# Two attentions on one core: one pair of value products moved in front of a step's second maxima, the other left behind its scores

## The chip, the core and the metric

The kernel runs on one core of a Trainium2 chip. A core has a matrix engine (TensorE, PE in the profile), three engines for elementwise work (VectorE or DVE, ScalarE or ACT, GpSimd or POOL), a queue that issues transfers (SP), an SBUF memory of 128 partitions and a PSUM memory of 128 partitions by 8 banks into which TensorE writes. The metric is the device time of one execution in microseconds (us), the median of several runs.

## The reference

The input is 16 sequences of 512 rows of 128 numbers. Four layers are applied one after the other, each to the layer norm of what came before it, and each added back: a causal attention of 16 heads of 8 numbers with a bias and a projection, a mixture of 8 experts of which two are taken per row, an attention of 16 heads without mask and projection, and a gated layer of width 352 with inputs and weights quantized to four-bit values. Only the attentions matter here:

```python
w = jnp.einsum('bhnd,bhmd->bhnm', q, k) * jax.lax.rsqrt(float(D))
w = jnp.where(mask > 0, w, NEG)          # first attention only
w = jax.nn.softmax(w, axis=-1)
attn = jnp.einsum('bhnm,bhmd->bhnd', w, v)
```

## The kernel before

Both attentions are one function, `attention`. Its unit of work is a *group* (batch b, group g): 16 batches of four groups, each of four heads. The four heads are numbered by a pair index i (0 or 1) and a half j (0 or 1); j says on which 64 partitions of `q` and `k` the head lies. A group takes four *steps*, kc = 0 to 3, one for each block of 128 keys.

In a step TensorE does three kinds of work, always in the order in which the program issues it (`mm` and `in_order`, line 294, tie each matmul to the one before).

- *Maxima* (`row_max`, its reduction is line 911): scores of one block of 128 queries, queries as rows, for a group three ahead (LEAD = 3), into a PSUM tile `ps_max` of two banks. VectorE reduces it to the largest score of each row. `ps_max`, `ps_d`, and in the first attention `ps_qk`, `ps_v` and others share a ring of two such tiles (`for_dve`). In the first attention a bf16 product with a mask follows each.
- *Scores* (`score`): scores of a block of keys against the queries, keys as rows, in one-bank tiles `ps_sc`. The maxima have been put into spare rows of `q`, so they are already subtracted. ScalarE takes the exponential of each tile into `pt` in SBUF (line 177), and in the first attention GpSimd clears what lies above the diagonal (line 969). `ps_sc`, `ps_av`, `ps_t`, `ps_mx`, and in the second attention `ps_qk` and `ps_v`, share a ring of four one-bank tiles (`for_act`).
- *Value products* (`attend`): `pt` times the values, for four heads, each 128 rows by 32 columns of the array, written to 32 partitions of one bank, `ps_av`, summed over the group's four steps. When the group is done, `leave` copies `ps_av` to SBUF on ScalarE, and later `divide` turns it back (`ps_d`) and divides.

Maxima and scores each come in `parts`: one part for each pair index i, thus two a step in the second attention, with 512 columns for each head. In the first attention only the causal part is computed; blocks of 512 and 384 columns (kc = 0 and 1) come in two parts, those of 256 and 128 (kc = 2 and 3) in one that holds both pairs.

The loop at the end of `attention` writes the order of a step out by hand. Small work that is due at a step (layer norm, turns, queries and keys, values, the gate) is kept in three tables by step: `soon` is done first, `later` after the first maxima and first scores, `last_of` after the second. A list `behind` holds work one step late: the value products of step kc are done at the end of the next step, when their exponentials have had time. So before the change a step is: `soon`; first maxima; first scores; (in step kc = 2 of the first attention, `divide`); `later`; second maxima; second scores; `last_of`; the four value products of the step before; at a group's end also `leave`. `last_of` holds the first attention's queries and keys (`both`, step 10 of 16), and in the second attention `divide` (step kc = 2).

Of the kernel before, what the change touches and what calls it, by code (L numbers as in the profile page):

```python
# [36 lines left out]
def transformer_kernel(  # L37
# [24 lines left out]
    B, S, E = x_in.shape  # L62
    NC = S // P
# [88 lines left out]
    def in_order(ins, queue="pe", passing=False):  # L152


        if queue in last:
            tc.add_manual_dep(
                ins.ins, last[queue].name,
                mybir.DependencyInfo(
                    mybir.DependencyClass.NoSync, mybir.DependencyReason.DATA
                ),  # L160
                reason="in_order",
            )
        if not passing:
            last[queue] = ins.ins
        return ins
# [127 lines left out]
    def mm(out, lhsT, rhs, start=True, stop=True):  # L293
        return in_order(nc.tensor.matmul(out, lhsT, rhs, start=start, stop=stop))  # L294
# [263 lines left out]
    def attention(layer):  # L558
# [25 lines left out]
        NP = 8  # L584
# [6 lines left out]
        def for_act(name):  # L591
            return ring["act"](name)
# [294 lines left out]
        def strip(j):  # L887
            return slice(64 * j, 64 * (j + 1))
# [52 lines left out]
        def main_parts(b, g):  # L941


            hv = halves[b, g // 2]
            va = state[b]["va"]
            pts = {}
            acc = {}

            def score(kc, pairs):
                q0 = kc * P if causal else 0  # L950
                n = S - q0
                m = len(pairs)
                tiles = [for_act("ps_sc") for j in range(2)]
                for u, i in enumerate(pairs):
                    p = 2 * (g % 2) + i
                    for j, ps in enumerate(tiles):
                        r = strip(j)
                        mm(
                            ps[:, u * n : (u + 1) * n],
                            hv["k"][r, p, kc * P : (kc + 1) * P], hv["q"][r, p, q0:S],  # L960
                        )
                for j, ps in enumerate(tiles):
                    pt = pool.tile([P, S], F32, tag="pt", name="pt", bufs=12 if causal else 8)
                    act.activation(pt[:, 0 : m * n], ps[:, 0 : m * n], AF.Exp, scale=SCALE)
                    if causal:

                        head = pt[:, 0 : m * n].rearrange("p (u n) -> p u n", u=m)[:, :, 0:P]
                        in_order(
                            nc.gpsimd.affine_select(  # L969
                                head, head, pattern=[[0, m], [1, P]], base=0,  # L970
                                channel_multiplier=-1, compare_op=ALU.is_ge, fill=0.0,
                            ),
                            queue="pool",
                        )
                    for u, i in enumerate(pairs):
                        pts[kc, i, j] = pt[:, u * n : (u + 1) * n]

            def attend(kc):
                if kc == 0:
                    acc[0] = for_act("ps_av")  # L980
                av = acc[0]
                q0 = kc * P if causal else 0
                for i in range(2):
                    for j in range(2):
                        s = 2 * j + i
                        mm(
                            av[32 * s : 32 * (s + 1), q0:S],
                            va[:, kc, NP * j + 2 * g + i, :],
                            pts.pop((kc, i, j)),
                            start=kc == 0, stop=kc == NC - 1,  # L990
                        )

            def leave():
                t = pool.tile([P, S], F32, tag="av_sb", name="av_sb")
                act.copy(t, acc.pop(0))
                return t

            return score, attend, leave

        def divide(b, g, t):  # L1000

            st = state[b]
            if g == 0:
                st["at"] = pool.tile([P, NC, E], F32, tag="at", name="at")
            ps = for_dve("ps_d")[:, 0, :]
            for c in range(NC):
                cols = slice(c * P, (c + 1) * P)
                turn_to(ps[:, cols], t[:, cols])
            p3 = ps.rearrange("p (n k) -> p n k", k=32)
            rec = pool.tile([P, NC * 4, 1], F32, tag="rec", name="rec")  # L1010
            vec.reciprocal(rec, p3[:, :, D : D + 1])
            at = st["at"].rearrange("p c (j n d) -> p (c j) (n d)", j=2, d=D)
            vec.tensor_tensor(
                at[:, :, 2 * D * g : 2 * D * (g + 1)].rearrange("p m (i d) -> p m i d", d=D),
                p3[:, :, 0:D].rearrange("p (m i) d -> p m i d", i=2),
                rec.rearrange("p (m i) o -> p m i o", i=2).to_broadcast([P, NC * 2, 2, D]),
                ALU.mult,
            )

        def turn_back(b):  # L1020
            if causal:
                state[b]["aT"] = transposed(pool, for_act, state[b]["at"], "aT", act.copy)
# [28 lines left out]
        def parts(blocks):  # L1051

            return [(0, 1)] if causal and 2 * blocks * P <= S else [(0,), (1,)]

        def max_steps(n):
            if n >= len(groups):
                return []
            b, g = groups[n]
            return [
                [(lambda c=c, u=u: row_max(b, g, c, u)) for u in parts(c + 1)]  # L1060
                for c in reversed(range(NC))
            ]
# [130 lines left out]
        behind, left = [], []  # L1193
# [53 lines left out]
        def quantize_after(b, step):  # L1247

            f = fp4_steps(b)
            for name, d in (  # L1250
                ("stats", 2), ("moments", 4), ("apply", 5), ("largest", 6), ("scale", 8),
                ("inverse", 10), ("scaled", 12), ("size", 14), ("least", 15), ("down", 15), ("grid", 16),
            ):
                later.setdefault(step + d, []).append(f[name])

        for n, (b, g) in enumerate(groups):
            nxt = n + LEAD
            steps = max_steps(nxt)
            score, attend, leave = main_parts(b, g)
            for kc in range(NC):  # L1260
                now = NC * n + kc
                maxima = steps.pop(0) if steps else []
                scores = [lambda u=u: score(kc, u) for u in parts(NC - kc)]
                for f in soon.pop(now, []):
                    f()
                if maxima:
                    maxima.pop(0)()
                scores.pop(0)()
                if kc == 2 and left:
                    bb, gg, t = left.pop(0)  # L1270
                    if not causal:
                        last_of.setdefault(now, []).append(lambda a=(bb, gg, t): divide(*a))
                    else:
                        divide(bb, gg, t)
                    if gg == G - 1 and causal:
                        later.setdefault(now + 1, []).append(lambda bb=bb: turn_back(bb))
                        at = now + 3
                        later.setdefault(at, []).append(lambda bb=bb: finish(bb))
                        gate_after(bb, at)
                    elif gg == G - 1:  # L1280
                        soon.setdefault(now + 1, []).append(lambda bb=bb: finish(bb))
                        quantize_after(bb, now + 1)
                for f in later.pop(now, []):
                    f()
                for f in maxima + scores:
                    f()
                for f in last_of.pop(now, []):
                    f()

                while behind:  # L1290
                    behind.pop(0)()
                behind.append(lambda kc=kc, f=attend: f(kc))
            behind.append(lambda b=b, g=g, f=leave: left.append((b, g, f())))
            max_done(nxt, NC * (n + 1))
        while behind:
# [290 lines left out]
    def gated_ffn():  # L1586
# [136 lines left out]
        fctx.close()  # L1723

    attention(0)

    later_pool = ctx.enter_context(tc.tile_pool(name="grids", bufs=1))
    grids = [later_pool.tile([P, NC, E], BF16, name=f"grid{b}") for b in range(B)]
    scales = [later_pool.tile([P, S // BLOCK, 1], F32, name=f"scale{b}") for b in range(B)]
    attention(1)  # L1730
    gated_ffn()

# [64 lines left out]
```

## Time and profile before

| | |
|---|---|
| median of 3 runs | 2253.49 us (2253.28 to 2253.72) |
| the profiled execution's own time | 2251.99 us |
| its span, first to last instruction | 2250.3 us |
| TensorE clock granted, mean | 0.964 of full |
| first attention, steady part | about 100 to 820 us |
| second attention | about 1220 to 2025 us |

The kernel's span has, in order, some 70 us of loading and the first attention's start, the first attention, the experts, the second attention, and the gated layer. In the profile's lines a group of instructions is named by engine, source line, operation and tile: `ps_av<-pt,va 128*32 128x512` is a product into `ps_av` that uses 128 rows and 32 columns of the array and streams 512 columns. In a listing by time, the first number is the start, the second the time until the end of the last of the merged instructions, `x8` how many there are; what stands in brackets is idle time of the engine ahead of it and what ended it. An fp32 matmul on TensorE leaves two records, so that four value products are `x8`.

### The profile page before, as it was taken

How to read it: one execution, taken by the hardware profiler on the slowest of the kernel's cores; microseconds unless marked ns; L12 is line 12 of the kernel's file. 1: busy time of each engine (PE TensorE's matmuls, PEld its weight loads, DVE VectorE, ACT ScalarE, POOL GpSimd, SP SyncE). 2: the span in 40 equal slices, each digit the busy share in tenths (PEclk: the TensorE clock that was granted, in tenths of full speed). 3: DMA queues.
4: the chain of work that ended last, by engine and by line, in shares of the span. 5: the costliest groups of instructions: out<-in, count | busy, mean ns of one | idle time of the engine just before them, and what ended most of it. 6: DMA issues, size and time to landing. Idle time of an engine off the chain costs nothing.

```text
span 2250.3 us, 38218 instructions
## 1 busy us (share of the span) xinstructions
PE 2025.0 (90%) x13140; PEld 1018.6 (45%) x13140; DVE 1649.7 (73%) x2994; ACT 1298.3 (58%) x2564; POOL 1022.3 (45%) x1641
## 2 busy tenths in 40 slices
PE   6999999999999965989998999999999999995887
PEld 3444444444444433655665433333333333333665
DVE  6667676777767757946434888888888888845887
ACT  1566556656556642323334777777777777782443
POOL 3444646566574663132202345555455454215554
PEclk6999999999999977999999999999999999997999
DMA  7311222322222103554553222322222222100000
GB/s 195 110 60 60 77 81 86 95 73 74 66 76 84 57 27 100 152 157 140 160 147 95 69 69 80 92 80 73 85 69 68 69 69 68 59 2 0 24 24 28
DMA packets 148736, 180.15 MB, mean 80 GB/s; under 512 B 25647, under 2 KB 112784, under 8 KB 140352
## 3 DMA queue, kind: packets, MB, share of 16 engines
q1 hardware_dynamic: 139614, 160.26, 23.8%
q0 software_dynamic: 8352, 17.20, 2.6%
q8 instruction: 105, 1.72, 0.3%
q14 instruction: 87, 0.71, 0.1%
q10 hardware_dynamic: 578, 0.26, 0.1%
HBM read 116.55 MB, written 58.99 MB: 78 GB/s over the span
## 4 chain that ended last, share of the span: by engine, by line
PE 37%; DVE 14%; ACT 4%; POOL 2%; issue 1%; DMA 0%; ACTq 0%; POOLq 0%
PE ps_av L294 10%; PE ps_sc L294 6%; PE ps_max L294 6%; DVE mx L911 5%; PE ps_h L294 4%; PE ps_y L294 4%; DVE hid L177 4%; ACT pt L177 3%; PE ps_d L297 2%; PE ps_qk L294 1%; POOL hid L177 1%; DVE f_mx L177 1%; PE ps_t L297 1%; DVE ml L177 1%; PE ps_v L294 1%
## 5 line engine op out<-in xcount | busy, mean ns | idle before, releaser
L911 DVE TENSOR_REDUCE mx<-ps_max 128x2 f32<-128x1024 f32 (+1 forms) x896 | 1005.4, 1144 | 259.4 <-PE ps_max L294 255.0
L177 ACT ACTIVATE pt<-ps_sc 128x512 f32<-128x512 f32 (+2 forms) x1792 | 895.9, 571 | 443.5 <-PE ps_sc L294 414.4
L294 PE MATMUL ps_sc<-q,k 64*128 64x512 f32 (+3 forms) x2048 | 480.9, 405 | 33.8 <-ACT pt L177 32.1
L294 PE MATMUL ps_av<-pt,va 128*32 128x512 f32 (+3 forms) x4096 | 482.5, 531 | 11.5 <-POOL pt L969 8.1
L294 PE MATMUL ps_max<-k,q 64*128 64x512 f32 (+3 forms) x2048 | 426.8, 433 | 26.3 <-DVE mx L911 19.2
L294 PEld LDWEIGHTS ps_max<-k,q 64*128 64x128 f32 x2048 | 185.9, 188 | 442.6 <-issue 174.6
L969 POOL TENSOR_SCALAR_AFFINE_SELECT pt<-pt 128x128 f32<-128x128 f32 (+1 forms) x768 | 245.8, 331 | 291.6 <-ACT pt L177 275.5
L294 PEld LDWEIGHTS ps_sc<-q,k 64*128 64x128 f32 x2048 | 230.6, 186 | 184.5 <-ACT pt L177 119.2
L1490 ACT ACTIVATE h<-ps_h,b1t 128x512 f32<-128x512 f32 x156 | 106.8, 687 | 192.3 <-PE ps_h L294 191.9
L1414 POOL DMA_INDIRECT got<-y_rows,backs x128 | 123.3, 964 | 99.3 <-DMA y_rows<-yt 63.4
L204 POOL TENSOR_TENSOR ln_rstd<-ln_ve,mhalf 128x4 f32<-128x4 f32 x62 | 63.7, 1028 | 204.2 <-DVE ln_nm L177 180.1
L294 PE MATMUL ps_y<-w2t,h 128*128 128x128 f32 x1248 | 149.6, 279 | 6.9 <-DVE yt L1504 6.9
L294 PE MATMUL ps_h<-xT,w1t 128*128 128x512 f32 x312 | 150.5, 615 | 3.0 <-issue 1.4
L294 PEld LDWEIGHTS ps_y<-w2t,h 128*128 128x128 f32 x1248 | 145.4, 195 | 9.6 <-DVE yt L1504 7.4
L294 PEld LDWEIGHTS ps_av<-pt,va 128*32 128x32 f32 x4096 | 86.5, 108 | 137.0 <-issue 79.5
L533 POOL DMA_INDIRECT x_rows<-xg,slots x128 | 126.6, 989 | 25.7 <-issue 21.6
L294 PE MATMUL ps_max<-mask_bf,ident_bf 128*128 128x128 bf16 (+1 forms) x768 | 126.9, 248 | 0.0
L177 DVE SCALAR_TENSOR_TENSOR hid<-f_a,hid 128x704 f32<-128x704 f32 x64 | 78.6, 1230 | 22.5 <-ACT f_a L177 22.4
L297 PE MATMUL ps_d<-cst,av_sb 128*128 128x128 f32 x512 | 84.1, 287 | 6.6 <-DVE mx L911 5.1
L294 PEld LDWEIGHTS ps_h<-xT,w1t 128*128 128x128 f32 x312 | 50.7, 191 | 77.1 <-ACT h L1490 52.0
L294 PE MATMUL ps_gu<-wgT,xqT 128*128 128x352 f32 x128 | 54.1, 506 | 32.7 <-DVE hid L177 32.7
L177 ACT COPY av_sb<-ps_av 128x512 f32<-128x512 f32 x128 | 76.3, 596 | 11.6 <-PE ps_av L294 2.8
(242 smaller groups left out, 2137.5 us busy)
## 6 DMA issues: line engine op xcount, KB each, us to landing
q<-d SPq DMA_DIRECT2D x256, 128.0 KB
k<-d SPq DMA_DIRECT2D x256, 128.0 KB
d<-hi SPq DMA_DIRECT2D x64, 256.0 KB
d<-lo SPq DMA_DIRECT2D x64, 256.0 KB
xt<-x_rows SPq DMA_DIRECT2D x39, 262.0 KB
w1t<-in_w_dram SPq DMA_DIRECT2D x39, 256.0 KB
w2t<-in_w_dram SPq DMA_DIRECT2D x39, 256.0 KB
y_rows<-yt SPq DMA_DIRECT2D x39, 256.0 KB
```

What stands on the lines that cost most here:

```text
L177: ins = f(*args, **kw)
L204: in_order(nc.gpsimd.tensor_tensor(rstd, ve, mhalf, ALU.pow), queue="pool")
L294: return in_order(nc.tensor.matmul(out, lhsT, rhs, start=start, stop=stop))
L297: return in_order(nc.tensor.transpose(out, src, ident))
L533: ins = in_order(nc.gpsimd.indirect_dma_start(out=x_rows[:, :], out_offset=bass.IndirectOffsetOnAxis(ap=slots[:, b0 + u, k, c : c + 1], axis=0
L911: nc.vector.tensor_reduce(hv["mx"][:, c, :, p0 : p0 + m], s4, AX.X, ALU.max),
L969: nc.gpsimd.affine_select(head, head, pattern=[[0, m], [1, P]], base=0, channel_multiplier=-1, compare_op=ALU.is_ge, fill=0.0,),
L1414: ins = in_order(nc.gpsimd.indirect_dma_start(out=got[:, c, :], out_offset=None, in_=y_rows[0 : min(NT, NE * (b + 1)) * TS, :], in_offset= ...
L1490: nc.scalar.activation(h[:, f, :], ps, AF.Gelu, bias=t["b1"][:, f : f + 1])
```

## The change

`attend` gets the pair index as an argument and does two products instead of four. A step's `behind` list now holds two entries (and `leave` at a group's end). The first is taken out behind `later` and in front of the second maxima, all others behind the second scores; `last_of` moves behind them. A step is now: `soon`; first maxima; first scores; (`divide`); `later`; two value products (i = 0) of the step before; second maxima; second scores; two value products (i = 1), at a group's end `leave`; `last_of`. In the steps kc = 2 and 3 of the first attention, which have no second part, the four products still stand side by side. In the program as built, the value products form 508 bursts of four before; after it 763 bursts of two and 127 of four, the rest at the edges. The instructions themselves, their number, their shapes and the transfers are the same.

```diff
-            def attend(kc):
-                if kc == 0:
+            def attend(kc, i):
+                if kc == 0 and i == 0:
                     acc[0] = for_act("ps_av")
                 av = acc[0]
                 q0 = kc * P if causal else 0
-                for i in range(2):
-                    for j in range(2):
-                        s = 2 * j + i
-                        mm(
-                            av[32 * s : 32 * (s + 1), q0:S],
-                            va[:, kc, NP * j + 2 * g + i, :],
-                            pts.pop((kc, i, j)),
-                            start=kc == 0, stop=kc == NC - 1,
-                        )
+                for j in range(2):
+                    s = 2 * j + i
+                    mm(
+                        av[32 * s : 32 * (s + 1), q0:S],
+                        va[:, kc, NP * j + 2 * g + i, :],
+                        pts.pop((kc, i, j)),
+                        start=kc == 0, stop=kc == NC - 1,
+                    )
...
                 for f in later.pop(now, []):
                     f()
+
+
+                if behind:
+                    behind.pop(0)()
                 for f in maxima + scores:
                     f()
+                while behind:
+                    behind.pop(0)()
                 for f in last_of.pop(now, []):
                     f()
-
-                while behind:
-                    behind.pop(0)()
-                behind.append(lambda kc=kc, f=attend: f(kc))
+                behind += [lambda kc=kc, f=attend, i=i: f(kc, i) for i in range(2)]
             behind.append(lambda b=b, g=g, f=leave: left.append((b, g, f())))
```

More of the change, by code (lines that the diff above doesn't have):

```diff
@@ L1284, in attention @@
                     f()
+                if behind:
+                    behind.pop(0)()
                 for f in maxima + scores:
-                    f()
-                for f in last_of.pop(now, []):
                     f()
@@ L1291, in attention @@
                     behind.pop(0)()
-                behind.append(lambda kc=kc, f=attend: f(kc))
+                for f in last_of.pop(now, []):
+                    f()
+                behind += [lambda kc=kc, f=attend, i=i: f(kc, i) for i in range(2)]
             behind.append(lambda b=b, g=g, f=leave: left.append((b, g, f())))
```

## The prediction, made before the changed kernel had run

> **What bounds the kernel now.** I read the busy times first, then the table of stages, then single steps in order of time, then the waits. Of the page and of the table of stages (busy us of each engine with its instructions, then TensorE clock, DMA share, GB/s):
>
> ```profile
> PE 2025.0 (90%) x13140; PEld 1018.6 (45%) x13140; DVE 1649.7 (73%) x2994; ACT 1298.3 (58%) x2564; POOL 1022.3 (45%) x1641
> ...
> L294 PE MATMUL ps_av<-pt,va 128*32 128x512 f32 (+3 forms) x4096 | 482.5, 531 | 11.5 <-POOL pt L969 8.1
> ```
>
> ```profile
> 100.00:820.00 720.00, 689.69 (x5326) 331.73 (x5324) 501.25 (x1100) 436.06 (x961) 408.29 (x970) 0.99 0.23 73
> 1220.00:2025.00 805.00, 756.70 (x4646) 300.98 (x4646) 678.04 (x1019) 621.44 (x1189) 364.25 (x408) 1.00 0.22 69
> ```
>
> The rows are the two attentions: TensorE is busy 96% and 94% of them, at nearly full clock, with VectorE at 70% and 84%. What the change touches is TensorE's queue alone, so I price it by the distance from one start in that queue to the next (ends are modelled, starts are not). One plain step of the second attention:
>
> ```profile
> 1622.28 0.50 PE L294 MATMUL ps_max<-k,q 64*128 64x512 f32 x2
> 1622.62 0.39 PE L294 MATMUL ps_sc<-q,k 64*128 64x512 f32 x2
> 1622.85 0.40 PE L294 MATMUL ps_max<-k,q 64*128 64x512 f32 x2
> 1623.08 0.39 PE L294 MATMUL ps_sc<-q,k 64*128 64x512 f32 x1
> 1623.69 0.49 PE L294 MATMUL ps_sc<-q,k 64*128 64x512 f32 x1 [0.23 <-ACT pt L177]
> 1624.11 1.07 PE L294 MATMUL ps_av<-pt,va 128*32 128x512 f32 x8
> 1625.11 0.50 PE L294 MATMUL ps_max<-k,q 64*128 64x512 f32 x2
> ```
>
> The step is 2.83 us. The fourth score starts 0.61 us after the third where two scores otherwise start together: its PSUM bank comes free only when ScalarE has done the step's first exponential (four banks, one held by ps_av). That is the stall the change can fill. The value products take 1.00 us to the next start. How are those eight records spread? Narrow windows of the same view show that, and so does one place in the first attention where only the first two of the four products could run, the others waiting for their mask:
>
> ```profile
> 1624.11 0.64 PE L294 MATMUL ps_av<-pt,va 128*32 128x512 f32 x4
> ```
>
> ```profile
> 764.68 0.62 PE L294 MATMUL ps_av<-pt,va 128*32 128x512 f32 x2
> ...
> 764.68 1.05 PE L294 MATMUL ps_av<-pt,va 128*32 128x512 f32 x4
> ```
>
> Each fp32 product leaves two records. The first passes of all four start within 0.02 us (four in the row of 0.64 us), the second passes 0.45 us later: the four run side by side, each in 32 columns of the array. The lone pair (two, then four records) has the same spacing and lasts 1.05 us, where the four last 1.07. **A pair costs what four cost.**
>
> **Second attention, part by part.** I take one batch, from its start at 1584.15 to the next at 1635.22: 51.07 us, 16 steps.
>
> Added: every step gets a second burst of value products, 16 x 0.995 = 15.92 us (0.995 is the distance from ps_av to the next ps_max, in 15 of 16 steps). Changes of shape on the array: in 10 of the steps the scores now precede value products (0.322 us from scores to ps_av) and no longer maxima (0.227), and second maxima follow value products (0.338 to their scores) and no longer scores (0.230): 10 x 0.095 + 9 x 0.11 = 1.9 us. In the other 6 steps a turn, values, queries or maxima's transpose lies there already, so only the burst is new.
>
> Removed: the stalls. In this batch the 12 distances from second scores to ps_av sum to 9.51 us where 12 x 0.322 = 3.86 is bare: 5.64 too much. The 4 in front of ps_d hold 1.13, the one in front of ps_v 0.32; ten from scores to maxima hold 0.83 and one from ps_av to maxima 0.63 (these two on VectorE). Sum 8.55. I take all of it as gone: with a burst of 1.0 us between first and second scores, each score's bank was used by scores one or two half steps of 1.65 us before, and its exponential is done about 1.05 us after them. VectorE needs 1.2 us for a maximum per half step of 1.65.
>
> Net 15.92 + 1.9 - 8.55 = +9.3 us a batch. Built from new: 32 half steps of 0.338 + 0.322 + 0.995 = 52.96, and what else the batch holds (four ps_d at 0.585, two ps_qk at 1.056, ps_v 1.088, ps_t 0.585, two ps_mx at 0.534: 7.2) is 60.2, or +9.1. With 9.2 for 61 of the 64 groups (61/4 = 15.25 batches): **+140**. The last three groups have no maxima; their steps of 2.27 to 2.61 become 2 x (0.322 + 0.995) = 2.63: +1.
>
> ps_d, behind the second burst now, costs the same 0.585 there, and its reader on VectorE has a half step until the second next maxima want its PSUM buffer. A new group's ps_av now asks for its bank earlier, and the built program lets it wait for the last exponential of the step before: done about 1.6 us after that score, wanted at 0.32 + 0.995 + 0.34 + 0.32 = 1.97. Nothing, with 0.4 us to spare. ScalarE's copy of the old ps_av still stands behind the second burst. No DMA is moved; the queues of SP, POOL and VectorE keep their order.
>
> **First attention.** Only half of its steps have second maxima: in these the value products are of 128 columns (step 0, 0.356 us to the next start) and 512 columns (step 1, 0.996).
>
> ```profile
> 422.57 0.43 PE L294 MATMUL ps_av<-pt,va 128*32 128x128 f32 x8
> 423.47 0.44 PE L294 MATMUL ps_max<-k,q 64*128 64x384 f32 x2 [0.47 <-DVE mx L911]
> ...
> 424.60 0.44 PE L294 MATMUL ps_max<-k,q 64*128 64x384 f32 x2
> ...
> 425.56 1.07 PE L294 MATMUL ps_av<-pt,va 128*32 128x512 f32 x8
> 426.56 0.38 PE L294 MATMUL ps_max<-k,q 64*128 64x256 f32 x2
> ```
>
> Eight groups from 406.8 (97.7 us) hold these distances. Added: step 0, four plain ones 0.431 + 0.356 - 0.337 + 0.106 = 0.56 each, and four with ps_mx already between, 0.356 each: 3.6. Step 1, six plain ones 0.371 + 0.996 - 0.281 + 0.105 = 1.19 each, two with ps_o between, 0.996 each: 9.1. Together 12.8. Removed: the bank wait in front of the 128-column products, 1.65 (four of eight are 0.36 too long); waits for VectorE's maxima in front of step 2, 2.05 of 3.2 (one alone is 2.9 and keeps 1.15); three smaller kinds within these steps, 2.0; half of the 0.9 in front of step 0; and 0.74 where the queries, now behind their step's value products, no longer wait for ps_d's buffer. Sum 6.9. Added wait: the first pair of step 0 comes some 0.9 us sooner after its mask on POOL. Set against where the masks end now, one group in eight would come 0.8 us too early, the others have 0.27 us or more; behind it on TensorE queue second maxima and scores. Net 12.8 - 6.9 + 0.8 = +6.7 for eight groups, x 61/8 = **+51**.
>
> **A rule of the Trainium skill** weighs in on the pair's price: "TensorE: Matmul & The Clock Gate", section "Measured speedup vs the span model". Its formula, span = one matmul + 4 ns for each further tile, leaves a pair at four's price and so speaks against this change. Its own measurement, three column tiles 2.38 times as fast, means 1.26 matmuls for three, or 0.13 for each further tile; an estimate from it is 1.13 for a pair and 1.39 for four, so 0.81 us against 0.995. By that a batch gains only 16 x (2 x 0.81 - 0.995) + 1.9 - 8.55 = +3.4 and eight groups +2.7, in all +72 and 2325. The lone pair of this trace says 1.05 against 1.07, at the same 512 columns, and I take that.
>
> **Sum.** 140 + 1 + 51 = +192 on the profiled execution's 2251.99 (span 2250.3): 2444. The median of the runs is 1.5 above it: **2445**.
>
> **The rivals.**
> (a) Faster: a pair takes half of four, 0.5 us, because two thirty-two column products share the array's input and not the time. Then the bursts cost nothing more, a batch changes by 1.9 - 8.55 = -6.65 (-101 in all) and eight groups by about -4.1 (-31): 2122. All of the change's sign hangs on that one price: each 0.1 us off it takes 2 x (244 + 61) x 0.1 + 4 = 65 us, so the break-even is near 0.995 - 192/650 = 0.70 us. For it: the records of one pair alone are few. Against: those say 1.05. Chance 3%.
> (b) Packing is less than perfect (0.81, above): 2325. Chance 6%.
> (c) The stalls return elsewhere: exponentials or maxima are late again because their work is merely moved. Then nothing is removed: 15.25 x 17.8 + 7.6 x 13.6 = +375, 2629. For it: ScalarE is 77% busy in the second attention. Against: its 39.3 us a batch spread over 60. Chance 4%.
> (d) The change does not do what it says: the scheduler keeps four together. The built program has 763 bursts of two where there were none, so no chance.
> The forecast's own case has 87%.
>
> **How the numbers follow.** Low end: a pair 0.05 us cheaper (half of 65, -33) and every stall of the first attention gone (2.4 more in eight groups, -18): about 2395. High end: 1 us a batch of stalls stays (+15) and only 4 of 6.9 go in the first attention (+22): about 2480. That leaves out (a), (b), (c) and a little of the main case: below 2 in 10. A measurement of this kernel can tell 0.2% (4.5 us) from no change. Faster 3%, within 0.2% 1%, slower 96%.
>
> **What would show it.** Right: plain steps of the second attention near 3.31 us, with ps_av twice a step, each as four records over 1.05 us, and the next start 0.99 after it; ps_max to the next batch near 60.2; the wait of ps_sc for ScalarE's exponential nearly gone; the first attention's eight groups near 104.4. Wrong: pairs whose second passes start 0.2 us after the first, or maxima that start before 0.9 us; or waits in front of ps_av for masks in more than one group of eight. The part between and behind the attentions should keep its length.

## The result and the profile after

The changed kernel takes 2493.38 us (2489.15 to 2496.74, four runs) against 2253.6: ratio 1.106, 95% interval 1.104 to 1.108. The direction was forecast, but the time lies 13 us above the range; the forecast +192 became +240. The page after, and the two attentions' stages (start:end, length, busy us with instructions of PE, PEld, DVE, ACT and POOL, granted clock, DMA share, GB/s; they lie later now):

```profile
PE 2311.1 (93%) x13140; PEld 1021.2 (41%) x13140; DVE 1678.9 (67%) x2994; ACT 1320.9 (53%) x2564; POOL 1023.3 (41%) x1641
...
L294 PE MATMUL ps_av<-pt,va 128*32 128x512 f32 (+3 forms) x4096 | 842.0, 533 | 9.5 <-POOL pt L969 8.6
```

```profile
100.00:840.00 740.00, 711.60 (x4796) 315.83 (x4794) 464.20 (x975) 394.83 (x861) 367.09 (x871) 0.94 0.22 69
1300.00:2210.00 910.00, 904.17 (x4498) 284.74 (x4498) 689.84 (x996) 603.31 (x1119) 356.73 (x399) 1.00 0.20 62
```

The same 4096 records of value products keep TensorE busy 842 us instead of 482, with nearly the same mean of one (533 ns, 531 before). In the second attention TensorE has almost no idle time left (busy 904 of 910 us). In the first its clock has fallen from 0.99 to 0.94.

By the first ps_v of the second attention (at 1341.8 us, before the change at 1237.8) the changed kernel is 104 us behind, and the rest of the program costs 138 more. The forecast was 51 and 141. So the second attention came as worked out, and the first cost twice as much. A plain step of the second:

```profile
1800.66 0.50 PE L294 MATMUL ps_max<-k,q 64*128 64x512 f32 x2
1800.99 0.40 PE L294 MATMUL ps_sc<-q,k 64*128 64x512 f32 x2
1801.32 1.05 PE L294 MATMUL ps_av<-pt,va 128*32 128x512 f32 x4
1802.30 0.50 PE L294 MATMUL ps_max<-k,q 64*128 64x512 f32 x2
...
1803.94 0.50 PE L294 MATMUL ps_max<-k,q 64*128 64x512 f32 x2
```

A burst of two is four records over 1.05 us, the next start comes 0.98 after it, and a step is 3.28 us. No score of this step waits for its bank.

The first attention has something new where its queries (ps_qk) are made. Ahead, before the change (two pieces of the listing by time), then after it:

```profile
428.70 1.98 PE L294 MATMUL ps_qk<-xnT,wp 128*128 128x512 f32 x4 [0.30 <-DVE mx L911]
430.62 0.85 PE L294 MATMUL ps_av<-pt,va 128*32 128x384 f32 x8
...
433.49 0.50 PE L294 MATMUL ps_max<-k,q 64*128 64x512 f32 x2 [0.39 <-DVE lo L177]
433.92 0.28 PE L294 MATMUL ps_max<-mask_bf,ident_bf 128*128 128x128 bf16 x2
434.13 0.50 PE L294 MATMUL ps_sc<-q,k 64*128 64x512 f32 x2
```

```profile
474.00 0.85 PE L294 MATMUL ps_av<-pt,va 128*32 128x384 f32 x8
474.78 1.98 PE L294 MATMUL ps_qk<-xnT,wp 128*128 128x512 f32 x4
...
479.56 0.70 PE L294 MATMUL ps_max<-k,q 64*128 64x512 f32 x2 [1.17 <-DVE lo L177]
480.20 0.40 PE L294 MATMUL ps_max<-mask_bf,ident_bf 128*128 128x128 bf16 x2
480.53 0.79 PE L294 MATMUL ps_sc<-q,k 64*128 64x512 f32 x2
```

The value products that stood behind the queries stand in front of them now. So the next maxima, which need the PSUM tile that ps_qk fills until VectorE has made `lo` of it, come 0.78 us sooner after ps_qk, and wait that much longer: 1.17 us of idle TensorE instead of 0.39. From there on the matmuls take longer: the scores of 512 columns 0.79 us, not 0.50. Three stretches of the table of busy times around it, with the columns named above:

```profile
469.30:479.70 10.40, 9.23 (x62) 3.74 (x60) 6.53 (x19) 4.69 (x11) 3.88 (x13) 1.00 0.13 49
479.70:489.90 10.20, 10.20 (x40) 3.53 (x40) 4.59 (x7) 3.97 (x8) 4.49 (x9) 0.50 0.48 154
489.90:500.10 10.20, 10.18 (x76) 4.21 (x74) 6.43 (x8) 7.43 (x17) 6.39 (x14) 1.00 0.43 128
```

The clock is half for 10.2 us, and TensorE has 40 records of matmuls where it has 76 next. Between 250 and 830 us the clock is halved eleven times, for 3.4 to 10.2 us each. Nine of these stretches begin 0.1 to 2.1 us after the end of such a wait; the two of 3.4 us begin within 0.3 us after a wait of 1.06 us for a mask.

### The profile page after: what moved, and what is told of

It is laid out like the page before. It is cut to its first block, busy times and chain, and to the rows that moved or that the text cites. A ratio compares the mean times of both kernels' runs of the same rounds, so it can differ in the third digit from the quotient of the medians.

```text
span 2491.8 us, 38219 instructions
## 1 busy us (share of the span) xinstructions
PE 2311.1 (93%) x13140; PEld 1021.2 (41%) x13140; DVE 1678.9 (67%) x2994; ACT 1320.9 (53%) x2564; POOL 1023.3 (41%) x1641
## 4 chain that ended last, share of the span: by engine, by line
PE 48%; DVE 6%; POOL 2%; ACT 1%; issue 0%; DMA 0%; ACTq 0%; POOLq 0%
PE ps_av L294 20%; PE ps_max L294 9%; PE ps_sc L294 5%; PE ps_h L294 4%; PE ps_y L294 4%; DVE hid L177 4%; PE ps_d L297 2%; PE ps_qk L294 1%; POOL hid L177 1%; DVE f_mx L177 1%; PE ps_t L297 1%; PE ps_v L294 1%; PE ps_mx L297 1%; DVE f_rc L177 1%; ACT f_a L177 1%; DVE f_sc L177 1%
## 5 line engine op out<-in xcount | busy, mean ns | idle before, releaser
L911 DVE TENSOR_REDUCE mx<-ps_max 128x2 f32<-128x1024 f32 (+1 forms) x896 | 1021.7, 1146 | 425.5 <-PE ps_max L294 417.9
L177 ACT ACTIVATE pt<-ps_sc 128x512 f32<-128x512 f32 (+2 forms) x1792 | 919.5, 566 | 671.3 <-PE ps_sc L294 663.6
L294 PE MATMUL ps_av<-pt,va 128*32 128x512 f32 (+3 forms) x4096 | 842.0, 533 | 9.5 <-POOL pt L969 8.6
L294 PE MATMUL ps_max<-k,q 64*128 64x512 f32 (+3 forms) x2048 | 450.1, 457 | 19.5 <-DVE lo L177 16.4
L294 PE MATMUL ps_sc<-q,k 64*128 64x512 f32 (+3 forms) x2048 | 398.3, 403 | 4.9 <-ACT pt L177 4.5
L294 PEld LDWEIGHTS ps_av<-pt,va 128*32 128x32 f32 x4096 | 135.6, 109 | 274.0 <-issue 223.2
L294 PEld LDWEIGHTS ps_sc<-q,k 64*128 64x128 f32 x2048 | 187.9, 189 | 89.7 <-issue 35.2
L873 POOL TENSOR_SCALAR q_a<-q_a 128x512 f32<-128x512 f32 x16 | 24.1, 1507 | 149.8 <-ACT q_a L177 149.8
L177 DVE RECIPROCAL rec<-ps_d 128x16 f32<-128x16 f32 x128 | 32.4, 253 | 79.0 <-PE ps_d L297 79.0
```

The lines of the kernel that those rows point to most:

```text
L177: ins = f(*args, **kw)
L873: nc.gpsimd.tensor_scalar(st["a"], st["a"], MAGIC, None, ALU.max), queue="pool"
L911: nc.vector.tensor_reduce(hv["mx"][:, c, :, p0 : p0 + m], s4, AX.X, ALU.max),
```

## The experiments

Two theories for the first attention's surplus: (1) the queries' move makes a wait, and the wait is followed by half clock; (2) bursts that use half of the array bring the clock down. I give the first attention as the time of eight groups in its steady part, twice the mean distance of ps_v over ten batches of four groups there: 98.8 us before, 113.0 after. A batch of the second attention is 50.9 before, 59.85 after.

**e1_queries_back**, against the changed kernel:

```diff
                 for f in maxima + scores:
                     f()
+                if causal:
+                    for f in last_of.pop(now, []):
+                        f()
                 while behind:
                     behind.pop(0)()
```

> The changed kernel, with one part undone: in the first attention the queries (and all of last_of) stand again in front of the last value products of their step; the value products stay split. Theory 1: the excess over my sum comes from the queries' move, by which the first maxima of the next step wait 1.24 us instead of 0.46 for their buffer, and each such wait is followed by 7 to 10 us at half clock. Then these half-clock stretches go and eight groups of the first attention take about 106 us instead of 113: total 2493 - 47 = about 2446. Theory 2: the half clock comes from the bursts of two products, which use half of the array. Then it stays, only 0.8 us per eight groups go, total about 2487.

Measured: 2462.95 us, ratio to before 1.092 (1.089 to 1.095); eight groups 107.3, second attention as in the changed kernel. Its waits (who waited for whom: us in total, times, longest) and its stretch of the first attention:

```profile
PE ps_max L294 <- DVE lo L177: 5.2, 13, 0.4
```

```profile
100.00:800.00 700.00, 681.61 (x4732) 306.63 (x4732) 458.11 (x969) 388.46 (x844) 360.13 (x856) 0.99 0.22 71
```

In the changed kernel the same row of waits is 15.2 us, 13 times, at most 1.2. The clock is back at 0.99 with the pairs still split, so theory 2 fails and theory 1 is borne out; 107.3 is near its 106, and 2463 lies 17 us above its total. 30 of the 240 us go with the queries' place, and that is too low: this edit doesn't only undo the move. It puts the queries between two pairs that stand side by side in the changed kernel, once in a batch:

```profile
410.47 0.84 PE L294 MATMUL ps_av<-pt,va 128*32 128x384 f32 x4
411.24 1.99 PE L294 MATMUL ps_qk<-xnT,wp 128*128 128x512 f32 x4
413.15 0.84 PE L294 MATMUL ps_av<-pt,va 128*32 128x384 f32 x4
```

One burst more is 0.77 us to the next start, an estimate of 12 us over the attention's 15.25 batches: most of the 17.

**e2_queries_only**, against the kernel before (`divide` of the second attention moves with the queries):

```diff
-                for f in last_of.pop(now, []):
-                    f()
-
                 while behind:
                     behind.pop(0)()
+                for f in last_of.pop(now, []):
+                    f()
```

> The kernel before, with only the queries (and the divide of the second attention) moved behind the step's four value products, which stay in one burst. Theory 1: the wait of 1.24 us appears and brings the half clock with it: eight groups of the first attention take 98.9 + 0.8 + about 5, total 2254 + 44 = about 2298. Theory 2: whole bursts keep the clock, total about 2260. A mixture (the wait starts the half clock, the pairs prolong it) would give stretches of 3.4 us and about 2270. The second attention should not move in any of them.

Measured: four runs, three of 2317.61 to 2322.09 and one of 2279.37, where the kernel before took 2256.4. The profiled one is of the three, and the numbers from its trace hold for them: eight groups 109.8.

```profile
PE ps_max L294 <- DVE lo L177: 15.2, 13, 1.2
```

```profile
100.00:800.00 700.00, 669.34 (x4654) 311.05 (x4650) 447.48 (x961) 377.95 (x827) 353.88 (x841) 0.87 0.22 70
```

With every burst whole, the wait is the same to a tenth, and the clock is 0.87, lower than with the split. Half clock begins 0.3 to 1.3 us after twelve of fourteen such waits. Theory 2 falls, and so does the mixture in which pairs prolong the half clock. The run of 2279 us is above the kernel before too, by 1.0%, and its clock over the whole program is 0.951 against 0.963 to 0.970. The cost is above theory 1's 44 us in three runs and below it in one; the three had the lower clocks, 0.928 to 0.940. Why they differ is open.

**e3_split_second_only**, against the changed kernel:

```diff
-                if behind:
+                if behind and not causal:
                     behind.pop(0)()
                 for f in maxima + scores:
                     f()
+                if causal:
+                    for f in last_of.pop(now, []):
+                        f()
```

> The split in the second attention alone; the first attention as in the kernel before. All theories: a batch of the second attention takes 59.85 us as in the changed kernel, the first attention 98.9 per eight groups as before, total 2254 + 135 = about 2389. If it is below 2370 or above 2405, the two attentions' costs do not simply add.

Measured: 2393.46, ratio 1.061 (1.059 to 1.064); eight groups 98.0, a batch 59.85. The second attention's split alone costs 137 us, the whole change 240, of which the first attention's part was 104: the two attentions' costs add.

**e4_late_whole_burst**, against the changed kernel. `behind` holds the step at which each entry is due; in the first attention both pairs come two steps late, in the second pair 0 one step and pair 1 two steps late. Either way one burst of four stands in front of the second maxima and none behind the scores:

```diff
-                if behind:
-                    behind.pop(0)()
+                while behind and behind[0][0] <= now:
+                    behind.pop(0)[1]()
...
-                while behind:
-                    behind.pop(0)()
...
-                behind += [lambda kc=kc, f=attend, i=i: f(kc, i) for i in range(2)]
+                behind.append((now + 1 + causal, lambda f=products: f(0)))
+                behind.append((now + 2, lambda f=products: f(1)))
+                behind.sort(key=lambda entry: entry[0])
```

> One burst of four value products stays, but stands in front of the second maxima. Second attention: pair 0 of the step before with pair 1 of the step before that, side by side. First attention: all four of two steps before. If a burst has one price whatever it holds, and what fills the stall is its place and not the split, then a batch of the second attention loses the waits for exponentials without paying a second burst: PE needs some 42 us, VectorE is busy 45, so about 46 instead of 51.0; the first attention loses 0 to 3 us per eight groups; total about 2170 (2140 to 2215). If filling the stall only moves it (rival c of the prediction), total stays within 10 us of 2254.

Measured: 2274.37, ratio 1.009 (1.006 to 1.011). The first attention gained, 94.1 for eight groups. The second lost: 54.0 a batch. Its listing by time shows why it did not gain:

```profile
1565.10 0.50 PE L294 MATMUL ps_max<-k,q 64*128 64x512 f32 x2
1565.44 0.39 PE L294 MATMUL ps_sc<-q,k 64*128 64x512 f32 x2
1565.66 0.40 PE L294 MATMUL ps_max<-k,q 64*128 64x512 f32 x2
1565.90 0.44 PE L294 MATMUL ps_sc<-q,k 64*128 64x512 f32 x1
1566.51 0.49 PE L294 MATMUL ps_sc<-q,k 64*128 64x512 f32 x1 [0.17 <-ACT pt L177]
1566.93 1.07 PE L294 MATMUL ps_av<-pt,va 128*32 128x512 f32 x8
```

The burst now parts first from second scores, and the second scores and the next step's first scores come 0.46 us apart; the fourth score waits for its bank as before. Four tiles of scores a step, three banks and one burst left one gap too short in both places of the burst. My expectation failed there, and its rival, that the stall only moves, held for the second attention. What the batch lost beyond that is on VectorE: between 1300 and 1900 us the waits for exponentials are 21.3 us (before 17.7), but the waits of maxima are

```profile
PE ps_max L294 <- DVE mx L911: 34.7, 56, 1.1
```

against 11.7 us before (and 4.4 for ps_d). `divide` now stands directly in front of the next maxima, which share its ring of two tiles. That this is the reason for most of these waits is read from the listing and was not tried alone.

**e5_first_late_whole**, the first attention of e4 with the second of the kernel before, and **e6_scores_first**, the same with this in the second attention:

```diff
+                if not causal:
+                    scores.pop(0)()
                 if maxima:
                     maxima.pop(0)()
-                scores.pop(0)()
+                if causal:
+                    scores.pop(0)()
```

> First attention as in e4_late_whole_burst (all four value products two steps late, in front of the second maxima, in one burst), second attention as in the kernel before. If the two attentions' costs add, as e3 had it, eight groups take 94.1 us and a batch of the second attention 50.9: total 2254 - 36 = about 2218. If the first attention's gain in e4 hung on anything in the second, it is lost and the total is near 2254.

> As e5_first_late_whole, and in the second attention a step begins with its first scores, followed by both maxima, the second scores and the whole burst. If the second attention's stall is the distance between first and second scores against the time of one exponential (about 1.02 us), then work that is there anyway fills it: the distance grows by the 0.23 us of one more pair of maxima, each of the 12 stalls of a batch shrinks by about as much, and a batch takes about 48.5 us instead of 50.9: total about 2218 - 37 = 2181. If VectorE, which then gets its two maxima of 1.2 us back to back, takes the place of the stall, the batch stays within 1 us of 50.9.

Measured: 2321.97 and 2317.04, where the kernel before took 2347.84 on that chip: ratios 0.989 (0.988 to 0.991) and 0.988 (0.986 to 0.990). The first attention is 94.1 in both. The second takes 57.3 a batch in both, though in e5 it is the kernel before's. Of e5, the stages, and one place of its listing:

```profile
100.00:770.00 670.00, 650.24 (x5184) 319.54 (x5179) 496.08 (x1045) 422.12 (x924) 394.35 (x935) 1.00 0.25 78
1260.00:2000.00 740.00, 660.00 (x3826) 261.97 (x3820) 582.39 (x881) 508.78 (x968) 322.12 (x364) 0.94 0.21 66
```

```profile
1417.02 0.58 ACT L177 COPY av_sb<-ps_av 128x512 f32<-128x512 f32 x1 [3.90 <-remote]
```

Once in most batches ScalarE stands idle for 3 to 4 us with no releaser in this core's records ("remote"), and half clock follows. No second attention in the traces of e1 to e4, all from one other chip, has such a row. The three runs that follow tell whether that is a matter of the chip; all are the same kernels again.

> The kernel of e5_first_late_whole again, since on the chip of that run the kernel before took 2348 us instead of 2254, with ScalarE idle for 3 to 4 us once in most batches of its second attention. On a chip where the kernel before takes about 2254: 2218 (ratio 0.984). On one like that chip: about 2322 again (ratio 0.989).

> The kernel of e6_scores_first again. On a chip where the kernel before takes about 2254: a batch of the second attention near 48.5 us and a total near 2181 if the distance between the scores sets the stall, near 2218 if VectorE takes its place. On a chip like that of e6: about 2317 again.

> The changed kernel itself, beside the two others on one chip. On a chip where the kernel before takes about 2254: 2493 (ratio 1.106). On a chip like that of e5, where the second attention of the kernel before carries idle time and half clock of its own: if its longer steps hide those ScalarE gaps, the changed kernel loses less and the ratio falls to about 1.07; if not, both grow and it stays near 1.10.

Measured, beside 2344.78 for the kernel before: 2319.95, ratio 0.990 (0.988 to 0.992); 2315.55, ratio 0.988 (0.986 to 0.990); the changed kernel 2564.84, ratio 1.094 (1.091 to 1.096), a batch of its second attention 64.9. Gaps of this kind are in these traces too. So the changed kernel's longer steps hide some of them, but not most: its batch grew by 5.1 us, that of e5 by 6.4.

Then the two kernels a third time, on the chip of e1 to e4:

> The kernel of e5_first_late_whole a third time, for a chip on which the kernel before takes about 2254: then 2218 (ratio 0.984). Where the kernel before takes about 2345: 2320 (0.990), as on two chips already.

> The kernel of e6_scores_first a third time. On a chip where the kernel before takes about 2254: a batch of the second attention near 48.5 us and a total near 2181 if the distance between first and second scores sets the stall, near 2218 if VectorE takes its place. Where the kernel before takes about 2345: 2316.

Measured, beside 2253.15 for the kernel before: 2229.16, ratio 0.990 (0.988 to 0.992), and 2214.23, ratio 0.983 (0.981 to 0.984). In e10 eight groups take 94.1 and a batch 50.9, as expected; the total fell by 24 instead of 36. The 4.7 us for eight groups hold in the steady part, 40 groups, and make 23.4 us there. They do not hold for the groups ahead of it: from the first ps_v to the steady part the kernel before took 140.4 us and e10 139.8. Two rows of e10's first attention, the wait behind the queries from 100 to 770 us and the stage, matter for the clock:

```profile
PE ps_max L294 <- DVE lo L177: 12.4, 13, 1.0
100.00:770.00 670.00, 649.94 (x5171) 319.25 (x5169) 495.28 (x1044) 422.39 (x923) 394.24 (x934) 1.00 0.25 78
```

Here too value products stand in front of the queries, and maxima behind them wait, with 0.96 us of idle TensorE each time. Not one of these waits is followed by half clock; so it is in the traces of e4 to e8 and e11 too. A wait a fifth shorter than the 1.17 us of the changed kernel left the clock alone, so theory 1 doesn't hold for every wait at this place.

In e11 a batch takes 50.0, not 48.5. The waits in the second attention from 1250 to 1900 us, of the kernel before and then of e11:

```profile
PE ps_sc L294 <- ACT pt L177: 19.3, 90, 0.2
PE ps_max L294 <- DVE mx L911: 11.7, 23, 0.6
PE ps_d L297 <- DVE mx L911: 4.4, 11, 0.4
```

```profile
PE ps_max L294 <- DVE mx L911: 20.9, 38, 0.7
PE ps_d L297 <- DVE mx L911: 10.4, 27, 0.4
```

The wait of scores for exponentials is out of the list, and the waits for VectorE's maxima have grown. VectorE, 86% busy, takes the place of most of the stall. e11 is the fastest version here, 1.7% under the kernel before.

## Why the prediction was right in direction and wrong in size, point by point

- **What bounds it.** Right. TensorE's queue set the time in both attentions.
- **A pair costs what four cost.** Right: 0.982 us to the next start where four took 0.995, and 0.342 against 0.356 for 128 columns. The 0.81 that I estimated from the table in the Trainium skill's "TensorE: Matmul & The Clock Gate", section "Measured speedup vs the span model" (rival b), is excluded; the formula there, 4 ns for each further tile, is nearer to these 13 to 14 ns for two further tiles.
- **Second attention, +141.** Right: +8.9 a batch (forecast 9.2), +138 with what follows; e3 alone gives +139 in its trace. The stalls are gone, as forecast, so rival (c) didn't come about; e4 shows the same stall coming back when the burst is not doubled.
- **The new ps_av bank.** Right: the second attention's waits have no row of ps_av for an exponential.
- **First attention, +51.** Wrong: +104. A term of the removed side failed: "half of the 0.9 in front of step 0". The term beside it, the 0.74 of the queries' own wait, came true: the row of ps_qk waiting for VectorE, 3.4 us between 100 and 820 us before, is gone. But I looked at the queries' own wait, and not at who takes the buffer that they fill. That wait of 0.46 us (beyond the bare distance) didn't halve; it grew by exactly the 0.78 us of value products that changed sides with the queries, to 1.24. In eight groups 0.92 became 2.48, where I had put 0.46: 2.0 us of the missing 7.5 (14.2 measured, 6.7 forecast). Most of the rest is half clock, for which my sum held no term. In the 40 groups of the steady part the clock is half for 81.9 us after and for 13.7 before. By the distances from start to start that fall in these stretches, against the same distances at full clock, that costs 5 to 6 us in eight groups, an estimate. e1 and e2, which take the move away and make it alone, show that wait and half clock both come with the move. That the wait's length brings the half clock is inferred from their order in time.
- **What stays open of it.** With the queries put back (e1) the first attention is 73 us slower than before, where my sum without both terms of the queries gives 51 + 7.6 x 1.2 = 60. The burst that e1 parts in each batch is some 12 of these 13 us. The sum fits better than its parts: eight groups would then take 108.2, measured were 107.3, and 4 us lie ahead of the steady part (59.4 us from the first ps_v to the second in e1, 55.4 before). That I can't assign.
- **A cause that I had wrong and a size that was right.** The wait of 2.9 us that I put down to VectorE is one for masks, in the middle of the burst, which the wait had already cut into two pairs:

```profile
472.13 1.30 PE L294 MATMUL ps_av<-pt,va 128*32 128x512 f32 x4
474.80 1.29 PE L294 MATMUL ps_av<-pt,va 128*32 128x512 f32 x4 [1.36 <-POOL pt L969]
```

  After the change 1.14 us of it stay, where I had 1.15.

## What to carry to other kernels

Products that run side by side in different columns of the array are paid as one burst, so parting them pays the burst again; it is worth it only where the gap to be filled is longer than the burst, and here it was at most 0.7 us, 0.47 on average, against 1.0. When a step is moved in a queue, follow the buffer that it fills to the next user of that buffer, for the distance that the move takes from it comes back as a wait. A filler between two ends of a ring mends one gap only: count the gaps of a period first, and look whether work that is there already (e11's maxima) can be put into them.

## What the runs showed of the hardware that I had not expected

- TensorE, over 95% busy in this stage, fell to half clock around waits of little more than 1 us. In the changed kernel nine of fourteen waits with 1.17 us of idle were followed by half clock of 6.8 or 10.2 us, in e2 twelve of fourteen, by up to 23.9. With 0.96 us of idle at the same place (e10 and the other runs with that first attention) none was. Length alone doesn't decide: five waits for masks with 1.36 us of idle, in the kernel before, were followed by none, and four of its five stretches of 3.4 us in this stage began 1.4 to 2.2 us after waits of only 0.47 us for maxima. What else decides was not tried. That the runs of one program, e2, took 2279 to 2322 us with different clocks suggests that the cost of such a wait is not fixed.
- On two of the three chips on which the first attention of e4 ran with the second of the kernel before (e5, e7, e10), that second attention took 57.3 us a batch instead of 50.9, with ScalarE idle for up to 4 to 5 us at a time for no reason in the profile, followed by half clock. The first attention took 94.1 us for eight groups on all three. The cause is open; ratios were taken on one chip each, and only they can be compared across chips.
